# Layer 0 of a four-layer image network: four products behind one attention step, loads behind the first stacks, scales moved by two products

## The chip, the core and the metric

The kernel runs on one core of a Trainium2 chip. The metric is the device time of one execution in microseconds (us); three runs of the kernel before took 3771.85, 3773.90 and 3775.54, median 3773.9.

The engines are named as in the profile: PE (TensorE, matrix products; PEld are its weight loads), DVE (VectorE), ACT (ScalarE, functions such as exp and Gelu, which need a table loaded), POOL (GpSimd), SP (SyncE, which here only issues DMA transfers). ACT and POOL can issue DMAs too. Each engine works through its own instructions in their order; a semaphore wait at the head holds up all that stands behind it. Results of PE go to PSUM, of which this part of the kernel uses four single banks for products and two double ones for scores.

## The reference

Eight images of 384 channels and 32 x 32 pixels pass through four residual layers. Only layer 0 is touched:

```python
x = x + L0(_gn(x))                      # group norm over 32 groups
def L0(x):
    q = dwproj(x, dw_q, g_q, b_q, pw_q) # and k, v alike
    attn = softmax(einsum('bhcn,bhcm->bhnm', q, k) * scale)   # 8 heads of 48
    out  = einsum('bhnm,bhcm->bhcn', attn, v)
    return bn(einsum('oc,bchw->bohw', w_out, out))
def dwproj(x, dw, g, b, pw):
    y = depthwise 3x3 convolution of x with dw
    y = gelu(bn(y, g, b))               # bn: mean and variance over all 8 images
    return einsum('oc,bchw->bohw', pw, y)
```

The batch norm inside `dwproj` needs all eight images' convolutions before the first Gelu. That splits layer 0 into two stages.

## The kernel before

All arithmetic is in 32-bit floats. The program is traced into instructions for five engines; a scheduler orders them within each engine by readiness and priority, and every DMA is put on one of eight semaphores in turn, so that a new DMA waits for the one before it on the same semaphore (the profile shows this as SP or ACT waiting for a DMA).

**Stage A, convolutions (0 to 384 us).** Image `b` is loaded (`load_x`), normed (`norm`: statistics on DVE, two tiny products with `g4` on PE, a power on POOL) and written by ACT into a padded tile `pad`, two of which take turns. The 3 x 3 convolution of q, k and v at once is done on PE by groups of 42 channels: `stack` copies three row-shifted versions of a group's channels out of `pad` into a tile `st` (three SP DMAs of 168 KB; six of 24 KB for the group of leftover channels, number NGC = 9), and six products with the weights `cw` (or `cwr` for group 9) sum the taps in PSUM. `groups[b]` says which groups an image does on PE, group 9 first; for even images the last three groups are done tap by tap on DVE instead (`convolve`, tile `yv`). ACT copies the sums to `y`, DVE takes statistics (`bn_stats`), and ACT issues three stores of `y` to the DRAM tensors `raw`. `stacks(AHEAD)` issues stacks nine work items ahead. Image 1 is loaded before image 0's stacks in SP's queue; the constants `gb0`, `sel0`, `sel1`, `msk`, `one3` come behind image 2.

**The passage (384 to 400 us).** `bn_params` makes one scale and one shift per channel in the layout of the groups (126 partitions by group). Six small products with selection matrices `sel0` and `sel1` move them into the layout of the images (`pmove`, lines 416 and 420), DVE masks and sums them into `ss0` (lines 426 to 435), and ACT's first Gelus read `ss0`. Meanwhile the attention's weights are loaded (line 512), and POOL clears two tiles `vt` for the values (`values_tile`, line 505).

**Stage B, attention (400 to 1840 us).** A step is a pair of key tiles: for image `b`, head pair `pr` (four), half of the queries `h` (two) and key tiles `kc`, `kc+1` there are 32 steps an image. Each step issues the scores of the next step (16 rows of PE, line 623, four at a time in quarters of the array), their exps on ACT (line 630), the Gelus due for the next image (`GELUS`, by step), and the weighing of its own probabilities (`weigh`, line 638, in quarters too) into two banks `pav`. Other work waits in a list `todo`: projections of q and k (line 558), values (line 531), out-projections (line 575), which use the whole array, three products each (two rows of the profile per product). Two of them are done behind every second step:

```python
            if n % NS or (b == 0 and pr == 0 and h == 0):
                for _ in range(min(2, len(todo))):
                    todo.pop(0)()
            if kc == NT8 - NS:
                normalise(b, pr, h, pav)
```

`normalise` divides by the sums on DVE and puts the result into `att`; for the last head pair by 12 small DMAs. The order on ACT in this stage is the program's own (`manual_schedule`); the other engines' follows it closely.

Behind it, layers 1 to 3 run to 3770 us; nothing of them changes.

Of the kernel before, what the change touches and what calls it, by code (L numbers as in the profile page):

```python
# [1 line left out]

# [50 lines left out]
def tile_kernel(ctx: ExitStack, tc: tile.TileContext, i: dict, out: bass.AP):  # L53
# [13 lines left out]
    def bank(name):  # L67
        return ps_mm.tile([P, HALF], F32, tag="mm", name=name)
# [11 lines left out]
    def load_const(name):  # L80
        src = i[name]
        t = const.tile(list(src.shape), F32, tag=name, name=name + "_sb")
        nc.sync.dma_start(out=t, in_=src)
        return t

    ident = load_const("ident")
    g4 = load_const("g4")
    mhalf = const.tile([P, 16], F32, name="mhalf")
    nc.vector.memset(mhalf, -0.5)
    ones = const.tile([P, P], F32, name="ones")  # L90
# [128 lines left out]
    with ExitStack() as pa:  # L219
# [20 lines left out]
            load_image(xts[b], x_img[b])  # L240

        load_x(0)
        cwr = load_a("cwr")
        cw = load_a("cw")
        cwv = load_a("cwv")
        vst = wa.tile([3 * GC, 3, 2, 6], F32, name="vst")

        def norm(b):
# [62 lines left out]
        def stack(b, g):  # L311

            padf = pads[b % 2].rearrange("p c h w -> p c (h w)")
            if g < NGC:
                st = sa.tile([3 * GC, H, W], F32, tag="st", name=f"st{b}_{g}")
                c, t = divmod(g, 3)
                for dy in range(3):
                    nc.sync.dma_start(
                        out=st[dy : 3 * GC : 3].rearrange("p h w -> p (h w)"),
                        in_=padf[t : 3 * GC : 3, c, dy * W : (dy + H) * W],  # L320
                    )
            else:
                st = sa.tile([32 + 3 * GR, H, W], F32, tag="sr", name=f"st{b}_{g}", bufs=2)
                for h in range(2):
                    for dy in range(3):
                        r = 32 * h + dy * GR
                        nc.sync.dma_start(
                            out=st[r : r + GR].rearrange("p h w -> p (h w)"),
                            in_=padf[3 * GC :, :, dy * W : (dy + H) * W],
                        )  # L330
            return st
# [2 lines left out]
        TAPS = [(1, 0, W, 0), (0, 0, W - 1, 1), (2, 1, W, 0)]  # L334
        AHEAD = 9
        groups = [(NGC, *range(NGC - 3 if b in ON_V else NGC)) for b in range(B)]
        work = [(b, g) for b in range(B) for g in groups[b]]

        begins = {max(2, work.index((b, NGC)) - AHEAD - 2): b for b in range(1, B)}
        sts, taps, todo, later, normed = {}, [], {}, list(work), {0}  # L340

        def stacks(n):
            while later and len(work) - len(later) < n and later[0][0] in normed:
# [2 lines left out]

        for f in norm(0):
            f()
        stacks(AHEAD)
        load_x(1)  # L350
        load_x(2)
        gb0 = load_a("gb0")
        sel0, sel1, msk, one3 = (load_a(n) for n in ("sel0", "sel1", "msk", "one3"))
        for n, (b, g) in enumerate(work):
            if n in begins:
                b2 = begins[n]
# [32 lines left out]
            for v in range(3):  # L389
                if g < NGC:  # L390
                    to, of = raw[v][b, g % 3 : 3 * GC : 3, g // 3, :], y[v : 3 * GC : 3, :]
                else:
                    to, of = raw[v][b, 3 * GC :, :, :], y[v * GR : (v + 1) * GR, :]
                nc.scalar.dma_start(out=to, in_=of)
            for _ in range(2):
                if taps:
                    taps.pop(0)()
# [4 lines left out]
        assert not taps and not todo and not xts  # L402


        scs, shs = bn_params(gb0[:, 0, :], gb0[:, 1, :], bn0)
        both = wa.tile([3 * GC, 2, NGC + 1], F32, name="both")
        nc.vector.tensor_copy(both[:, 0, :], scs)
        nc.vector.tensor_copy(both[:, 1, :], shs)
        rest = wa.tile([3 * GR, 2, KC], F32, name="rest")
        nc.vector.tensor_tensor(  # L410
            rest, both[: 3 * GR, :, NGC:].to_broadcast([3 * GR, 2, KC]),
            one3.unsqueeze(1).to_broadcast([3 * GR, 2, KC]), ALU.mult,
        )
        pm = bank("pmove").rearrange("p (a v n) -> p a v n", a=2, v=4)
        for v in range(3):
            nc.tensor.matmul(
                pm[:, 0, v, : 2 * (NGC + 1)], lhsT=sel0[:, v, :],
                rhs=both.rearrange("p s g -> p (s g)"), start=True, stop=True,
            )
            nc.tensor.matmul(  # L420
                pm[:, 1, v, : 2 * KC], lhsT=sel1[:, v, :],
                rhs=rest.rearrange("p s k -> p (s k)"), start=True, stop=True,
            )
        got = wa.tile([P, 3, 2, KC, 3], F32, name="got")
        for v in range(3):
            nc.vector.tensor_tensor(
                got[:, v], pm[:, 0, v, : 2 * (NGC + 1)].rearrange("p (s g) -> p s g", s=2)[
                    :, :, :NGC
                ].rearrange("p s (k t) -> p s k t", t=3),
                msk.unsqueeze(1).unsqueeze(1).to_broadcast([P, 2, KC, 3]), ALU.mult,  # L430
            )
        nc.vector.reduce_sum(
            ss0.rearrange("p v s k -> p (v s k)"), got.rearrange("p v s k t -> p (v s k) t"), AX.X
        )
        nc.vector.tensor_tensor(
            ss0.rearrange("p v s k -> p v (s k)"), ss0.rearrange("p v s k -> p v (s k)"),
            pm[:, 1, :3, : 2 * KC], ALU.add,
        )

# [50 lines left out]
    with ExitStack() as pb:  # L492
# [9 lines left out]

        def values_tile(s):
            t = wb.tile([P, NT8, 2 * NH0, 32], F32, name=f"vt{s}")
            nc.gpsimd.memset(t, 0.0)
            nc.gpsimd.memset(t[:, :, :, HQ0 : HQ0 + 1], 1.0)
            vts.append(t)

        values_tile(0)
        for v, nm in enumerate(("wq0", "wk0", "wv0")):  # L510
# [1 line left out]
            nc.sync.dma_start(out=t, in_=i[nm])  # L512
            w_in.append(t)
        wo0 = wb.tile([P, KC, C], F32, name="wo0_sb")
        nc.sync.dma_start(out=wo0, in_=i["wo0"])
        rec = wb.tile([P, B * NU, 16], F32, name="rec")

        qks, atts = {}, {}
# [1 line left out]

        GELUS = {
            s: [divmod(i, KC) for i in range(2 * k, min(2 * k + 2, 3 * KC))]
            for k, s in enumerate((7, 9, 11, 13, 17))
        }

        def values(b, t):
            pv = bank(f"pv{b}_{t}")
# [39 lines left out]
        def out_project(b, m, h):  # L569
            hs = slice(h * HALF, (h + 1) * HALF)  # L570
            xh = op.tile([P, HALF], F32, tag="xh", name=f"xh{b}_{m}_{h}")
            nc.sync.dma_start(out=xh, in_=x_img[b][:, m, hs])
            po = bank(f"po{b}_{m}_{h}")
            for c in range(KC):
                nc.tensor.matmul(  # L575
# [94 lines left out]
        for n, (b, pr, h, kc) in enumerate(steps):  # L670
# [39 lines left out]
            for k in range(NS):  # L710
                weigh(b, pr, kc + k, pav, cur[k])

            if n % NS or (b == 0 and pr == 0 and h == 0):
                for _ in range(min(2, len(todo))):
                    todo.pop(0)()
            if kc == NT8 - NS:
                normalise(b, pr, h, pav)
# [1046 lines left out]
def _layouts(a):  # L1764
# [33 lines left out]
        gb[: 3 * GR, k, NGC] = v[:, NGC * GC :].reshape(-1)  # L1798
    L["gb0"] = gb

    sel = np.zeros((GC, 3, 3, P), f)
    for v in range(3):
        for t in range(3):
            sel[np.arange(GC), v, v, 3 * np.arange(GC) + t] = 1
    L["sel0"] = sel.reshape(3 * GC, 3, P)
    sel = np.zeros((3, P - 3 * GC, KC, 3, P), f)
    for v in range(3):
        for q in range(P - 3 * GC):
            sel[v, q, :, v, 3 * GC + q] = 1
    L["sel1"] = sel.reshape(3 * GR, 3, P)  # L1810
    row = np.arange(P)[:, None]
    L["msk"] = ((row % 3 == np.arange(3)) & (row < 3 * GC)).astype(f)
    L["one3"] = np.tile(np.eye(KC, dtype=f), (3 * GR // KC, 1))

    hrow = np.arange(C).reshape(NH0, HD0)
    rows = np.concatenate(
# [65 lines left out]
```

## Time and profile before

| What | us |
|---|---|
| median of three runs | 3773.9 |
| the profiled execution | 3772.1 |
| its span | 3770.3 |
| PE busy (97%) | 3647.7 |
| DVE busy | 1818.9 |
| ACT busy | 1316.8 |
| first convolution product starts | 21.9 |
| last convolution product ends | 384.5 |
| first projection starts | 400.4 |
| distance of images 1 to 6 in stage B | 177.4 |

In a line of the timeline stand start and duration in us, engine, line of the code, operation, output and inputs, number of instructions, and in brackets how long the engine had been idle and what released it. In a line of the waits: who waited for whom, total us, times, longest. A busy PE is not PE at its peak, since its rows overlap; the distance of starts tells more. The row PEclk is the clock granted to PE in tenths; at half speed a row of 512 columns starts 0.83 us behind the one before, at full speed 0.43.

### The profile page before, as it was taken

The page shows a single profiled execution, that of the slowest core. Times are in us where ns is not written, and L with a number is a line of the kernel's source. Part 1 is how long each engine was busy: PE and PEld are TensorE (multiplying, and loading weights), DVE is VectorE, ACT ScalarE, POOL GpSimd, SP SyncE. Part 2 cuts the span into 40 slices and gives each one's busy share as a digit, 9 for nine tenths or more (in the row PEclk, how much of TensorE's full clock was granted, in tenths as well). Part 3 has the DMA queues.
Part 4 walks back from the last instruction along what each step waited for, and adds up shares of the span by engine and source line. Part 5 has one row for each costly group of instructions (what it writes and reads, how often), then busy time and mean ns, then how long its engine had stood idle before and what let it go on. Part 6 is the DMA issues. An engine that isn't in the chain of part 4 may idle for free.

```text
span 3770.3 us, 39346 instructions
## 1 busy us (share of the span) xinstructions
PE 3647.7 (97%) x15754; PEld 1521.3 (40%) x15754; DVE 1818.9 (48%) x2841; ACT 1316.8 (35%) x1564; POOL 194.8 (5%) x153
## 2 busy tenths in 40 slices
PE   7999899999999999999799999999999999999898
PEld 3444333333333333333244534445444444444433
DVE  5876223232323232323346557565664666547664
ACT  2222364554545454534222321323222232322222
POOL 0000000000000000000000010200102010010111
PEclk9999999999999999999899999999999999999898
DMA  6777311111212020212340000100001001010000
GB/s 201 240 245 245 107 50 37 65 44 55 61 41 74 25 74 26 72 27 71 138 183 25 26 34 17 34 34 17 34 17 49 19 17 34 17 51 17 1 34 18
DMA packets 83097, 242.64 MB, mean 64 GB/s; under 512 B 18336, under 2 KB 18864, under 8 KB 82520
## 3 DMA queue, kind: packets, MB, share of 16 engines
q1 hardware_dynamic: 69894, 200.56, 16.1%
q10 hardware_dynamic: 13008, 39.43, 3.1%
q8 instruction: 128, 2.10, 0.2%
q14 instruction: 67, 0.55, 0.0%
HBM read 122.78 MB, written 75.50 MB: 53 GB/s over the span
## 4 chain that ended last, share of the span: by engine, by line
PE 40%; DVE 9%; ACT 1%; issue 0%; POOL 0%; DVEq 0%; POOLq 0%; ACTq 0%
PE y L1265 11%; PE ph L1244 8%; DVE y L1339 6%; PE pq L1384 3%; PE pw L1347 3%; PE pf L1650 3%; PE s L1545 3%; PE pav L1561 2%; PE pss L1587 1%; DVE hd L1230 1%; DVE off L1454 1%; PE pk L1519 1%; PE pv L1528 1%; PE xsb L1505 1%; PE plog L1007 1%; PE pom L1467 1%
## 5 line engine op out<-in xcount | busy, mean ns | idle before, releaser
L630 ACT ACTIVATE p<-s 128x1024 f32<-128x1024 f32 x512 | 496.4, 1021 | 496.9 <-PE s L623 496.5
L1265 PE MATMUL y<-hd,w_sb 128*128 128x512 f32 x1080 | 491.0, 600 | 3.6 <-DVE hd L1230 3.6
L638 PE MATMUL pav<-p,vt 64*64 64x512 f32 x4096 | 486.6, 590 | 0.0
L1244 PE MATMUL ph<-h,w_sb 128*128 128x512 f32 x1104 | 483.3, 594 | 0.0
L623 PE MATMUL s<-qk,qk 48*64 48x512 f32 x3072 | 372.7, 600 | 4.4 <-ACT p L630 4.4
L381 PE MATMUL pk<-st,cw_sb 126*126 126x512 f32 x720 | 316.4, 600 | 5.2 <-DVE ga_a L118 4.2
L1244 PEld LDWEIGHTS ph<-h,w_sb 128*128 128x128 f32 x1104 | 207.6, 190 | 253.1 <-issue 250.3
L1265 PEld LDWEIGHTS y<-hd,w_sb 128*128 128x128 f32 x1080 | 199.3, 191 | 249.8 <-issue 236.0
L638 PEld LDWEIGHTS pav<-p,vt 64*64 64x64 f32 x4096 | 156.2, 133 | 285.4 <-issue 285.1
L595 DVE COPY ta<-pav 128x512 f32<-128x512 f32 x64 | 44.3, 691 | 439.2 <-PE pav L638 439.2
L1339 DVE SCALAR_TENSOR_TENSOR y<-h,tap,y 128x992 f32<-128x992 f32 (+1 forms) x192 | 233.8, 1241 | 1.6
L1454 DVE SCALAR_TENSOR_TENSOR off<-q,dw_sb,off 128x225 f32<-128x225 f32 (+3 forms) x432 | 213.3, 549 | 1.7
L1254 ACT ACTIVATE hd<-ph,b_sb 128x512 f32<-128x512 f32 x180 | 122.7, 682 | 258.3 <-PE ph L1244 257.9
L381 PEld LDWEIGHTS pk<-st,cw_sb 126*126 126x126 f32 x720 | 137.6, 193 | 176.8 <-issue 167.8
L623 PEld LDWEIGHTS s<-qk,qk 48*64 48x64 f32 x3072 | 102.5, 132 | 241.5 <-issue 184.6
L78 DVE COPY qk<-pq 128x512 f32<-128x512 f32 x48 | 33.2, 691 | 293.6 <-PE pq L558 281.8
L387 ACT COPY y<-pk 126x512 f32<-126x512 f32 (+1 forms) x136 | 75.9, 584 | 250.7 <-PE pk L381 118.3
L1552 ACT ACTIVATE p<-s 128x1024 f32<-128x1024 f32 x96 | 93.1, 1021 | 173.4 <-PE s L1545 173.3
L575 PE MATMUL po<-att,wo_sb 128*128 128x512 f32 x288 | 135.7, 621 | 8.5 <-DMA att<-al 8.5
L1230 DVE TENSOR_TENSOR hd<-hd,cb 128x512 f32<-128x512 f32 x180 | 122.2, 684 | 35.4 <-ACT hd L1254 35.0
L1347 PE MATMUL pw<-y,upw 128*128 128x512 f32 x288 | 129.7, 603 | 7.6 <-DVE y L1339 7.6
L558 PE MATMUL pq<-g,wq_sb 128*128 128x512 f32 x288 | 132.8, 612 | 2.2 <-ACT g L483 2.2
(278 smaller groups left out, 4004.4 us busy)
## 6 DMA issues: line engine op xcount, KB each, us to landing
g<-raw SPq DMA_DIRECT2D x72, 512.0 KB
st<-pad SPq DMA_DIRECT2D x180, 168.0 KB
raw<-y ACTq DMA_DIRECT2D x180, 168.0 KB
xa<-in_x_dram SPq DMA_DIRECT2D x24, 512.0 KB
xh<-in_x_dram SPq DMA_DIRECT2D x48, 256.0 KB
f<-in_x_dram SPq DMA_DIRECT2D x24, 512.0 KB
f<-o SPq DMA_DIRECT2D x24, 512.0 KB
o<-ot SPq DMA_DIRECT2D x42, 256.0 KB
```

The costliest lines, as they stand in the source:

```text
L381: nc.tensor.matmul(pk[h].rearrange("p (h w) -> p h w", w=W)[: 3 * nch, :, o0 : o0 + c1 - c0], lhsT=lhs, rhs=rhs, start=(k == 0), stop=(k = ...
L558: nc.tensor.matmul(pq, lhsT=w_in[v][:, c, pr * P : (pr + 1) * P], rhs=acts[b][v][:, c, h * HALF : (h + 1) * HALF], start=(c == 0), stop=(c ...
L575: nc.tensor.matmul(po, lhsT=wo0[:, c, m * P : (m + 1) * P], rhs=atts[b][:, c, hs], start=(c == 0), stop=(c == KC - 1),)
L623: nc.tensor.matmul(s[64 * k : 64 * k + 64, j * HALF : (j + 1) * HALF], lhsT=kt[r, k0 : k0 + 64], rhs=qt[r, h * HALF : (h + 1) * HALF], sta ...
L630: nc.scalar.activation(p, s, AF.Exp, scale=scale)
L638: nc.tensor.matmul(pav[k][64 * j : 64 * j + 64, :], lhsT=vts[b % 2][r, kc, 2 * hd : 2 * hd + 2, :].rearrange("p a b -> p (a b)"), rhs=p[r, ...
L1230: nc.vector.tensor_tensor(hd, hd, state["cb"], ALU.mult)
L1244: nc.tensor.matmul(ph, lhsT=w1[:, e, c, dc * P : (dc + 1) * P], rhs=state["h1"][c], start=(c == 0), stop=(c == KC - 1),)
L1265: nc.tensor.matmul(y, lhsT=w2[:, e, dc, m * P : (m + 1) * P], rhs=state[h, k], start=(k == 0), stop=(k == NE * KC - 1),)
L1339: nc.vector.scalar_tensor_tensor(d, f, tap2[:, c, t : t + 1], d, ALU.mult, ALU.add)
L1347: nc.tensor.matmul(pw[h], lhsT=upw2[:, c, m * P : (m + 1) * P], rhs=y[c][:, hs], start=(c == 0), stop=(c == KC - 1),)
L1454: nc.vector.scalar_tensor_tensor(d, f, dw3[:, t : t + 1], d, ALU.mult, ALU.add)
```

## The change

- `ident` and `g4` are no longer loaded first. `g4` and the first third of `cw` come behind image 0, then `cwv` and `cwr`.
- Image 0 does groups 0, 1 and 2 before group 9. Image 1's load, the rest of `cw` and `ident` are held behind the first two groups' stacks (`issue_after`).
- `sel0`, `sel1` and `one3` have new contents, and `is_v` is new. In the changed program's order on SP, the small constants (`gb0`, `sel0`, `sel1`, `msk`, `is_v`, `one3`, and stage B's `gbo`, `gw`, `gbias`, `ewt`, `sel2`) stand before the first stack.
- The last image's groups 5, 6 and 7 are stored from POOL's queue, not from ACT's.
- Scales and shifts are spread over q, k and v by a mask on DVE (`both`, `rest`), and two products move all of them, instead of six.
- POOL's clearing of `vt` waits until the scales are done.
- The first image's loads `xh` wait behind `wo0`.
- Gelus of the next image come three at a time at steps 9, 13 and 17, not two at a time at 7, 9, 11, 13 and 17.
- Up to four items of `todo` are done behind the second of four steps; the very first unit keeps two behind each.

```diff
-    ident = load_const("ident")
-    g4 = load_const("g4")
...
         load_x(0)
+        g4 = load_const("g4")
+        cw = wa.tile([3 * GC, NGC, 3, 3 * GC], F32, name="cw_sb")
+        nc.sync.dma_start(out=cw[:, :3], in_=i["cw"][:, :3])
+        cwv = load_a("cwv")
         cwr = load_a("cwr")
-        cw = load_a("cw")
-        cwv = load_a("cwv")
...
-                    nc.sync.dma_start(
+                    stacked[0] = nc.sync.dma_start(
...
+        groups[0] = (*groups[0][1:4], NGC, *groups[0][4:])
...
+        stacks(2)
+        with tc.issue_after(stacked[0].ins):
+            load_x(1)
+            nc.sync.dma_start(out=cw[:, 3:], in_=i["cw"][:, 3:])
+            ident = load_const("ident")
         stacks(AHEAD)
-        load_x(1)
         load_x(2)
...
-                nc.scalar.dma_start(out=to, in_=of)
+                queue = nc.gpsimd if b == B - 1 and g in (5, 6, 7) else nc.scalar
+                queue.dma_start(out=to, in_=of)
...
+        both = wa.tile([3 * GC, 3, 2, NGC], F32, name="both")
+        rest = wa.tile([3 * GR, 3, 2, KC], F32, name="rest")
+        two = bn_params(gb0[:, 0, :], gb0[:, 1, :], bn0)
+        for k, t in enumerate(two):
+            sh = [3 * GC, 3, NGC]
+            nc.vector.tensor_tensor(
+                both[:, :, k], t[:, :NGC].unsqueeze(1).to_broadcast(sh),
+                is_v.unsqueeze(2).to_broadcast(sh), ALU.mult,
+            )
...
-        for v in range(3):
-            nc.tensor.matmul(
-                pm[:, 0, v, : 2 * (NGC + 1)], lhsT=sel0[:, v, :],
...
+        nc.tensor.matmul(
+            pm[:, :nv], lhsT=sel0, rhs=both.rearrange("p v s g -> p (v s g)"),
+            start=True, stop=True,
+        )
+        nc.tensor.matmul(
+            pm[:, nv : nv + 6 * KC], lhsT=sel1, rhs=rest.rearrange("p v s k -> p (v s k)"),
+            start=True, stop=True,
+        )
...
-            nc.gpsimd.memset(t, 0.0)
+            zero = nc.gpsimd.memset(t, 0.0)
+            tc.add_manual_dep(
+                zero.ins, scales.ins.name, mybir.DependencyInfo(
+                    mybir.DependencyClass.Sync, mybir.DependencyReason.DATA
+                ), reason="scales first",
+            )
...
-            s: [divmod(i, KC) for i in range(2 * k, min(2 * k + 2, 3 * KC))]
-            for k, s in enumerate((7, 9, 11, 13, 17))
+        GELUS = {s: [(v, c) for c in range(KC)] for v, s in enumerate((9, 13, 17))}
...
-            nc.sync.dma_start(out=xh, in_=x_img[b][:, m, hs])
+            with tc.issue_after(w_last.ins) if b == 0 else nullcontext():
+                nc.sync.dma_start(out=xh, in_=x_img[b][:, m, hs])
...
-            if n % NS or (b == 0 and pr == 0 and h == 0):
-                for _ in range(min(2, len(todo))):
+            early = b == 0 and pr == 0 and h == 0
+            if early or kc == NS:
+                for _ in range(min(2 if early else 4, len(todo))):
                     todo.pop(0)()
```

## The prediction

> **What bounds the kernel now.** First the page: span, engine totals, the slices.
>
> ```profile
> span 3770.3 us, 39346 instructions
> PE 3647.7 (97%) x15754; PEld 1521.3 (40%) x15754; DVE 1818.9 (48%) x2841; ACT 1316.8 (35%) x1564; POOL 194.8 (5%) x153
> ...
> PE   7999899999999999999799999999999999999898
> ...
> PEclk9999999999999999999899999999999999999898
> ```
>
> TensorE (PE) is busy throughout; the thin slices are the start, the passage from stage A to the attention (380 to 400 us) and two places behind it that the change leaves alone. So time comes from PE's waits, and from what PE does between waits. Second, PE's waits, longest first:
>
> ```profile
> PE gna_a L116 <- DVE mv_a L110: 11.4, 2, 10.2
> PE pmove L416 <- DVE both L408: 10.5, 1, 10.5
> PE pk L381 <- DMA st<-pad: 10.5, 2, 9.9
> PE po L575 <- DMA att<-al: 8.5, 4, 4.9
> ```
>
> Only some 40 us in all: two at the start, one in the passage, one at the attention's end. Third, the timeline of the first 31 us and of the passage:
>
> ```profile
> 4.56 1.39 SPq L171 DMA_DIRECT2D xa<-in_x_dram  x3
> 14.36 1.73 SPq L318 DMA_DIRECT2D st<-pad  x2
> 21.93 8.15 PE L381 MATMUL pk<-st,cwr_sb 18*18 18x512 f32 x12 [9.89 <-DMA st<-pad]
> ...
> 386.95 0.59 ACT L387 COPY y<-pk 126x512 f32<-126x512 f32 x1 [2.30 <-DMA raw<-y]
> ...
> 391.08 3.51 POOL L505 MEMSET vt<- 128x4096 f32 x1
> ...
> 391.46 3.16 DVE L407 COPY both<-bnsc_qkv 126x10 f32<-126x10 f32 x1
> ...
> 400.40 1.22 PE L558 MATMUL pq<-g,wq_sb 128*128 128x512 f32 x1 [2.16 <-ACT g L483]
> ```
>
> The first stack is issued at 14.36, but image 1 (4.56) and the 1.7 MB of `cw` stand before it in SP's queue: the queue's packets finish with image 1 at 18.66, and only then does the stack move. In the passage, a 126x10 copy that takes 0.17 elsewhere takes 3.16, as long as POOL's memset beside it. Fourth, PE inside the attention:
>
> ```profile
> 1007.18 2.00 PE L623 MATMUL s<-qk,qk 48*64 48x512 f32 x16
> 1009.00 1.90 PE L638 MATMUL pav<-p,vt 64*64 64x512 f32 x16
> 1010.83 5.42 PE L575 MATMUL po<-att,wo_sb 128*128 128x512 f32 x12
> 1016.18 1.95 PE L623 MATMUL s<-qk,qk 48*64 48x512 f32 x16
> ```
>
> There is no wait, yet starts are not evenly spaced. Scores and weighing run as quartets 0.429 apart, full products 0.429 apart. From the rows' single starts: last weighing quartet to first full product 0.538, that one to the second 0.534, last full product to scores 0.522, first score quartet to the second 0.480. Against even spacing, one change to full products and back costs 0.109 + 0.105 + 0.093 + 0.051 = 0.358 us, the same to 0.01 in the 93 batches from 480 to 1780 us (values' products, 0.323 apart, show the same surplus).
>
> **The change part by part.** *Four products behind one step.* Work is equal; only the number of batches falls. In the changed program's order of PE they go from 102 to 59: six fewer in each of images 1 to 6, four in image 0, three in image 7. 36 x 0.358 = 12.9 for images 1 to 6. Elsewhere scores that follow weighing directly lie at 0.429, so nothing returns. The exception is behind Gelu batches: scores two steps later start at 0.51 with two quartets at 0.48, 0.187 together. Gelu batches fall from five to three: 6 x 2 x 0.187 = 2.2. Together 15.1. The bounds: all new successions late leaves 36 x 0.171 = 6.2; none late gives 18.5.
>
> Banks: `pav` holds two of four, so the third product needs the first one's bank. The second product's 2.57 us covers one 0.69 evacuation, even behind a Gelu batch. Four out-products need 4 x 2.8 of DVE (copy 0.69, statistics 0.69, 0.73, 0.69), 11.2 against PE's 10.3; the third still finds its bank.
>
> *Gelu in threes.* ACT's rows in image 0:
>
> ```profile
> 470.58 1.28 ACT L483 ACT_TABLE_LOAD   x1
> 471.88 2.37 ACT L483 ACTIVATE g<-g,ss 128x1024 f32<-128x1024 f32 x2
> 474.27 1.28 ACT L630 ACT_TABLE_LOAD   x1
> ```
>
> A batch costs 2 x 1.28 + 3 x 1.18 = 6.1 instead of 4.9. Behind a batch of products (5.2 us or more) it is covered. Image 0's fourth unit has none: there PE waited 2.25 before, and with three Gelus I get 2.25 + 1.2 = 3.5. But the batch at 470 moves to a step with four products, so its wait of 2.1 to 2.3 and the half-speed products behind it (7.15 with the other wait) fall away. I give back half the slow phase (1.3): 7.15 - 3.5 - 1.3 = 2.3, lateness 0.2, four batches 1.4: image 0 saves 3.9.
>
> *Image 7.* Three batches fewer, -1.1. But its third early out-product ran after the last weighing (1823.07, 2.84 us), while PE waited for `att` until 1830.86. Now it comes before that weighing, so the last normalisation starts 2.6 later: +1.5 net. Attention: -15.1 - 3.9 + 1.5 = -17.5.
>
> *Loads behind the first stacks.* Without `ident` ahead and with `g4` behind, image 0 arrives 0.9 earlier, so `pad`'s first chunk is ready at 13.4; three stack DMAs go out 0.8 apart, and the last lands 2.4 after issue (40.67 to 43.08 shows that on an empty queue): 17.6, 4.3 earlier. Image 1, two thirds of `cw` and `ident` (2.8 MB, 8.5 us at the 330 GB/s seen here) now precede the third stack: it lands near 30.9, when two groups are done: 0.9 of waiting. Group 9 needs a bank that ACT frees behind a store of `yv`, whose taps DVE finishes near 39.5: another 1.5. Bounds of this feeding: 0 and 6.
>
> At the start products run at 0.83, half speed, from 21.93 to 34.20, costing 5.1. *The Trainium skill*, "TensorE: Matmul & The Clock Gate", Part 1, says that full clock comes after one busy window of about 3.4 us; by the rule the cold cost would be 1.7, by the row 5.1, for products with 18 rows. The phase from 400.40 to 406.3, with full products, is nearer to what now starts: 5.9 us, 2.9 lost. I take that: -2.2.
>
> Eleven small loads (`gb0` to `sel2`) are now issued before the first stack, in SP's idle time. Before, five held SP from 49.75 to 57.9 while image 1's stacks waited, and PE lost 7.1 between 63 and 78 us (starts against 0.43: waits of 2.3, then slow clock). I credit 2 of it, bounds 0 and 7. Stage A: -4.3 - 2.2 + 2.4 - 2.0 = -6.1.
>
> *The passage.* PE's last product ends at 384.45. ACT's last copy waited behind stores until 386.95: with three groups' stores on POOL it starts at 384.7 (-2.25). The memset now waits for the scales, so DVE's 3.1 stall goes (-3.0); four fewer move products x 0.53 and one `got` instead of three, less two more small DVE operations: -1.5. The first product comes at 393.65, 6.75 earlier; I take -6.7. Weights must be there: `wq` landed at 394.28, but was issued at 390.14, after the last of six `g` loads had landed; now it is queued right behind them and should land near 391. If not, 0.6 is lost. The memsets end near 400, the first `vt` copy needs them at 409: covered. `xh` behind `wo0`: needed only in image 1, free.
>
> Nine stores on POOL: no row shows one. The skill's "SBUF — State Buffer" (the "DVE blocks DMA" trap) speaks against it: descriptors of such a DMA can't be written while DVE holds a shared port, 0.62 becoming 3.1 us. Three stores of the last group queue before POOL's power (387.0 in the new chain): at 1 us each they are out by 383, by the rule at 3.1 each 390, a loss of 3. DVE's rows here are statistics of 0.69 and 0.57, no copies; I take no loss and keep 3 for the range.
>
> Sum: -6.1 - 6.7 - 17.5 = -30.3. The profiled execution took 3772.1, its span 3770.3; the median is 3773.9. From the median: **3743.6 us**.
>
> **Rivals.** *The stacks eat the head start*: the third one and the bank cost 6, the boundary gains nothing: -24, 3750. For it: SP waits for ACT's stores already at 33.43 and 40.67; against: no PE wait there so far. *The switch is dear only where a wait stands*: new successions late: -9 less, and POOL's stores cost 3: -18, 3755. For it: the 0.51 rows; against: all those follow Gelus. *The boundary clears wholly*: -36, 3738. *Slower*: a merged batch's third product waits for its bank because DVE's copy stands behind the 2.8 us chain of the one before. From 0.7 us per batch on (43 x 0.7 = 30) the gain is gone; at a full 1.4 it is 3774 - 30 + 60 = 3804. Against: 2.57 of cover. *Nothing moves*: PE's time is products alone, and the gaps come back elsewhere: 3773.
>
> **How the numbers follow.** Likeliest 50% (alone 3737 to 3749), stacks 18%, dear switch 13%, boundary 14%, slower 3%, nothing 2%. The range 3735 to 3756 takes in the first four. 0.2% (7.5 us) is about what a measurement of this kernel can tell from no change: faster 0.95, same 0.02, slower 0.03.
>
> **What would show it.** First stack product near 17.6; first `pq` about 13 before 400.4; no 3 us copy beside the memset; images 1 to 6 174.9 us apart instead of 177.39; 12 or more rows between weighing and scores doubled to 24 with the same 0.358. Wrong if PE waits for `st` or banks before 60 us, if POOL's power comes late, or if merged batches show a gap inside.

## The result, and the profile after

The changed kernel takes 3751.11 us (median, 3749.07 to 3757.77) where the kernel before takes 3772.88: a ratio of 0.9948, 95% interval 0.993 to 0.9967. It is faster by about 20 us, not by the 30.3 of the sum. Its profiled execution took 3751.05, its span is 3749.3, 21.0 under the 3770.3 before; the points below are made on these two spans. First the page's span and PE's rows of the slices:

```profile
span 3749.3 us, 39325 instructions
PE 3632.0 (97%) x15746; PEld 1533.0 (41%) x15746; DVE 1820.6 (49%) x2840; ACT 1280.2 (34%) x1536; POOL 199.5 (5%) x162
...
PE   7999999999999999999799999999999999999888
...
PEclk8999999999999999999899999999999999999898
```

The busy products fell by only 16 us of 3648. PE's waits of the changed kernel:

```profile
PE gna_a L114 <- DVE mv_a L108: 14.2, 2, 9.0
...
PE po L590 <- DMA att<-al: 11.6, 4, 7.9
PE pk L391 <- DMA st<-pad: 10.2, 3, 7.2
```

The passage's wait of 10.5 is gone from the top of this list. The wait for the first stack is 7.2 instead of 9.9, but there are now three such waits instead of two, and the wait of `gna_a` for `mv_a`, which was 11.4, has grown to 14.2, 5.2 of it late in stage A. The timeline of the changed kernel, start and passage:

```profile
13.16 4.90 SPq L318 DMA_DIRECT2D st<-pad  x6
18.00 12.85 PE L391 MATMUL pk<-st,cw_sb 126*126 126x512 f32 x24 [7.17 <-DMA st<-pad]
18.11 1.51 SPq L169 DMA_DIRECT2D xa<-in_x_dram  x3
22.63 8.10 SPq L318 DMA_DIRECT2D st<-pad  x3
32.95 6.98 PE L391 MATMUL pk<-st,cw_sb 126*126 126x512 f32 x12 [2.10 <-DMA st<-pad]
...
387.75 0.58 ACT L397 COPY y<-pk 126x512 f32<-126x512 f32 x1 [1.94 <-PE pk L391]
...
392.29 0.18 DVE L423 TENSOR_TENSOR both<-bnsc_qkv,is_v_sb 126x27 f32<-126x27 f32 x1
...
396.36 8.18 PE L572 MATMUL pq<-g,wq_sb 128*128 128x512 f32 x12 [2.20 <-DMA wq_sb<-in_wq_dram]
```

The first stack product comes at 18.00 (before 21.93). PE waits for the third stack at 32.95, and its next twelve products take 6.98 instead of 5.3. At stage A's end ACT's last copy follows PE directly, `both` takes 0.18, and the first `pq` comes at 396.36 (before 400.40). And one place in the attention (image 3):

```profile
997.38 1.90 PE L653 MATMUL pav<-p,vt 64*64 64x512 f32 x16
999.20 5.42 PE L590 MATMUL po<-att,wo_sb 128*128 128x512 f32 x12
1004.46 5.31 PE L572 MATMUL pq<-g,wk_sb 128*128 128x512 f32 x12
1009.70 1.95 PE L638 MATMUL s<-qk,qk 48*64 48x512 f32 x16
```

Two out-products and two projections now stand in one batch; the 24 rows run without a gap, so the third product finds its bank.

Against the sum, on the profiled spans:

| part | predicted | measured | from |
|---|---|---|---|
| stage A, start of its last product | -6.1 | +3.3 | 383.87 to 387.13 |
| passage, from there to the first `pq` | -6.7 | -7.3 | 16.53 to 9.22 |
| first `pq` to first scores | 0 | -0.05 | 15.24 to 15.19 |
| first scores to `gmean` (layer 0 over) | -17.5 | -15.9 | 1431.31 to 1415.41 |
| behind it | 0 | -1.1 | 1923.39 to 1922.32 |

One line carries nearly all of the miss: stage A.

### The profile page after: what moved, and what is told of

Same layout as the page of the kernel before. It is cut to its first block, busy times and chain, and to the rows that moved or that the text cites. A ratio compares the mean times of both kernels' runs of the same rounds, so it can differ in the third digit from the quotient of the medians.

```text
span 3749.3 us, 39325 instructions
## 1 busy us (share of the span) xinstructions
PE 3632.0 (97%) x15746; PEld 1533.0 (41%) x15746; DVE 1820.6 (49%) x2840; ACT 1280.2 (34%) x1536; POOL 199.5 (5%) x162
## 4 chain that ended last, share of the span: by engine, by line
PE 40%; DVE 9%; ACT 1%; issue 0%; DMA 0%; POOL 0%; DVEq 0%; POOLq 0%; ACTq 0%; SPq 0%
PE y L1281 11%; PE ph L1260 8%; DVE y L1355 6%; PE pq L1400 3%; PE pw L1363 3%; PE pf L1666 3%; PE s L1561 3%; PE pav L1577 2%; PE pss L1603 1%; DVE hd L1246 1%; DVE off L1470 1%; PE pk L1535 1%; PE pv L1544 1%; PE xsb L1521 1%; PE pom L1483 1%; PE plog L1023 0%
## 5 line engine op out<-in xcount | busy, mean ns | idle before, releaser
L590 PE MATMUL po<-att,wo_sb 128*128 128x512 f32 x288 | 132.8, 615 | 11.6 <-DMA att<-al 11.6
```

What stands on the lines that cost most here:

```text
L590: nc.tensor.matmul(po, lhsT=wo0[:, c, m * P : (m + 1) * P], rhs=atts[b][:, c, hs], start=(c == 0), stop=(c == KC - 1),)
```

## The experiments

Each ratio is to runs of the kernel before on the same chip, whose medians lay between 3772.9 and 3777.2 us; times of kernels that ran on different chips are best compared by their ratios. "Last product" is the start of stage A's last product; the passage runs from there to the first `pq`; the attention from the first scores to `gmean`. All in us, each from one profiled execution; the ratio is that of the timed runs.

| kernel | first product | last product | passage | attention | ratio to before, 95% |
|---|---|---|---|---|---|
| before | 21.93 | 383.87 | 16.53 | 1431.31 | |
| after | 18.00 | 387.13 | 9.22 | 1415.41 | 0.9948 (0.993, 0.9967) |
| e1 attention alone | 21.93 | 382.18 | 16.97 | 1415.55 | 0.9953 (0.994, 0.9967) |
| e2 passage alone | 21.83 | 382.75 | 10.10 | 1431.13 | 0.9978 (0.9969, 0.9987) |
| e3 start alone | 18.20 | 385.94 | 15.29 | 1429.79 | 0.9998 (0.9989, 1.0006) |
| e4 after, old start | 22.05 | 381.43 | 9.06 | 1415.05 | 0.9927 (0.9913, 0.994) |
| e5 after, four stacks first | 18.33 | 380.36 | 9.06 | 1414.36 | 0.9929 (0.9916, 0.9943) |
| e6 after, tail and Gelu moved | 18.19 | 385.50 | 9.38 | 1395.97 | 0.9893 (0.9877, 0.9908) |
| e7 after, stores on ACT | 18.53 | 387.75 | 11.41 | 1414.21 | 0.9944 (0.9929, 0.9959) |
| e8 after, memset free | 18.32 | 389.56 | 9.06 | 1414.13 | 0.9938 (0.9923, 0.9954) |
| e9 batches alone | 22.23 | 386.69 | 16.82 | 1459.11 | 1.0066 (1.005, 1.0083) |
| e10 before, copies as products | 22.40 | 390.18 | 14.47 | 1433.36 | 0.999 (0.9981, 0.9998) |
| e11 e6 with the old start | 22.21 | 383.78 | 9.06 | 1395.60 | 0.9886 (0.987, 0.9903) |
| e12 e6 with four stacks first | 18.75 | 382.31 | 9.06 | 1395.49 | 0.9885 (0.9869, 0.9902) |

### Which part brings what: e1 to e4

Attention alone (e1), on the kernel before:

```diff
-            s: [divmod(i, KC) for i in range(2 * k, min(2 * k + 2, 3 * KC))]
-            for k, s in enumerate((7, 9, 11, 13, 17))
+        GELUS = {s: [(v, c) for c in range(KC)] for v, s in enumerate((9, 13, 17))}
...
-            if n % NS or (b == 0 and pr == 0 and h == 0):
-                for _ in range(min(2, len(todo))):
+            early = b == 0 and pr == 0 and h == 0
+            if early or kc == NS:
+                for _ in range(min(2 if early else 4, len(todo))):
```

> The kernel before with two edits alone: up to four products behind one step of four, and Gelu in threes. If the cost of a change to full products and back is what the batches save, images 1 to 6 last 174.88 us each instead of 177.39 (-15.1 in all), image 0 saves 1.6 to 3.9 and the tail loses 1 to 1.5: time near 3773 - 16 to -17.5, 3756. If the switch is dear only where a wait stands, images last about 176.4 and the time is near 3764.

Measured 3755.53 against 3777.2. Images 1 to 6 last 174.89 each, the attention 15.8 less. The theory holds; the rival of a dear switch is out.

Passage alone (e2): the scales by two products, the memset's wait, the nine stores on POOL, as in the change.

> The kernel before with the passage's edits alone: scales by two products, the memset behind the scales, nine stores on POOL. The theory: last conv product to first pq falls from 15.95 to about 8.7 us, stage A's end does not move, time near 3773 - 7 = 3766. The rival, that POOL's stores hold up its power: the passage falls by 4 only, 3769.

Measured 3766.39; the passage is 10.10 (in this profile PE waited 3.1 for `wq`; it is 9.06 in the profiles where `wq` was there in time). The theory holds: 6.4 of some 7, and POOL's stores cost nothing.

Start alone (e3):

```diff
-    ident = load_const("ident")
-    g4 = load_const("g4")
...
+        groups[0] = (*groups[0][1:4], NGC, *groups[0][4:])
...
+        stacks(2)
+        with tc.issue_after(stacked[0].ins):
+            load_x(1)
+            nc.sync.dma_start(out=cw[:, 3:], in_=i["cw"][:, 3:])
+            ident = load_const("ident")
         stacks(AHEAD)
-        load_x(1)
```

> The kernel before with the start's edits alone: loads behind the first stacks, group 9 fourth, cw in two parts. The theory: the first product comes 3.9 us earlier, but the wait for the third stack and the image boundaries, which run in another planned order on DVE, ACT and SP, give back more than that: stage A's last product ends 3 us later than in the kernel before (near 387.7), time near 3776. The rival of the prediction: the head start lasts, the last product ends near 378.5 and the time is near 3767. A third: the loss belongs to another edit, and this one ends near 381.

Measured 3775.07 against 3777.2: no difference, within -4 and +2. The last product starts 2.1 later than in the profile of the kernel before, though the first one comes 3.7 earlier. The prediction's own figure (3767) is out. The expected loss of 3 did not show in the time: the profiled execution was the fastest of 13, its passage and first projections were 2.6 shorter than in the kernel before, and why is not known.

The changed kernel with these edits undone (e4):

> The changed kernel with the start's edits undone. The theory: stage A's last product ends at 384.4 as in the kernel before, 3.3 us earlier than in the changed kernel; time near 3751 - 3 = 3748. The rival, that the start's edits are worth 6 us as predicted: near 3757.

Measured 3747.67, 0.9927: not slower than the changed kernel, so the start's edits are not worth 6 us there either. Attention and passage alone add to 26.1 by their ratios, and e4 saves 27.6. The start adds nothing that these times can show.

### Where the head start goes: e5, and all profiles side by side

Stage A wanders between executions, so I took all profiles with the same start together: seven with the old one, five with the new (after, e3, e6, e7, e8), two with four stacks first. Mean start of the n-th product of stage A (12 to a group), and the new start's lead over the old:

| product | old | new | new - old | four - old |
|---|---|---|---|---|
| 1st | 22.08 | 18.25 | -3.8 | -3.5 |
| 19th | 34.57 | 28.05 | -6.5 | -6.3 |
| 25th (third stack) | 37.09 | 33.39 | -3.7 | -6.3 |
| 37th (group 9, new start) | 42.28 | 39.66 | -2.6 | +1.7 |
| 61st | 52.67 | 52.35 | -0.3 | +3.9 |
| 85th (image 1) | 63.95 | 63.70 | -0.3 | +3.0 |
| 97th | 73.87 | 70.12 | -3.7 | -2.9 |
| 145th | 96.26 | 92.53 | -3.7 | -2.7 |
| 193rd | 118.71 | 119.22 | +0.5 | -2.0 |
| 481st | 240.08 | 240.49 | +0.4 | -1.9 |
| 577th | 285.87 | 288.82 | +3.0 | -2.6 |
| last | 384.41 | 387.18 | +2.8 | -3.1 |

Up to the 241st product the standard deviation within the old and the new start is 0.2 to 1.5 us; at the end it is 3.0 (old) and 1.6 (new), so the last row alone would prove little. The rows above it show where the lead is spent: 2.8 at the third stack, 1.1 of slow clock behind that wait, 2.3 around group 9, then 3.5 won at the border to image 1, 4.2 lost near product 170 and 2.5 near product 577.

At the last two PE's `gna_a`, the small product in the norm of the next image but one, waits for that image's statistics on DVE. In DVE's timeline of the changed kernel near 280 us, image 7's statistics (`st_a`, six, then `mv_a`) stand among taps of image 6:

```profile
276.98 1.29 DVE L103 BATCH_NORM_STATS2 st_a<-xa 128x6 f32<-128x512 f32 x2 [7.43 <-DMA xa<-in_x_dram]
...
278.62 1.28 DVE L103 BATCH_NORM_STATS2 st_a<-xa 128x6 f32<-128x512 f32 x2
279.82 0.73 DVE L290 TENSOR_SCALAR yv<-xn,cwv_sb 126x1024 f32<-126x1024 f32 x1
...
284.55 0.68 DVE L103 BATCH_NORM_STATS2 st_a<-xa 128x6 f32<-128x512 f32 x1
285.15 1.20 DVE L292 SCALAR_TENSOR_TENSOR yv<-xn,cwv_sb,yv 126x961 f32<-126x961 f32 x1
...
288.06 0.30 DVE L108 BATCH_NORM_AGGREGATE mv_a<-st_a 128x2 f32<-128x36 f32 x1
```

Four taps and five statistics of products stand between the first `st_a` and `mv_a`, 11.1 us in all; `gna_a` waits 5.2 us at 288.50. The diff has no line there: the planner, given another start, put DVE's work in another order. With the old start the six stand together and take 5.5 to 7.0 from the first to `mv_a`, and `gna_a` waits 0.3 at most; in all five profiles with the new start they take 10.8 to 12.2, and it waits 4.4 to 7.5. At image 3 (product 170) the new order puts `mv_a` behind two more of image 0's taps, and the wait is 2.4 to 4.3 instead of 1.2 to 1.7.

It is tempting to call this order the cause, but at image 7 the old start pays one step later. Its PE passes `gna_a` and then waits 1.6 to 5.6, in six profiles for `ga_a`, which DVE makes of that product, and in one (e9) for a store. PE in e10, with the old start, and in the changed kernel:

```profile
285.62 0.35 PE L116 MATMUL gna_a<-mv_a,g_sb 128*128 128x2 f32 x2
291.60 7.14 PE L381 MATMUL pk<-st,cw_sb 126*126 126x512 f32 x12 [5.63 <-DVE ga_a L118]
...
288.50 0.56 PE L114 MATMUL gna_a<-mv_a,g_sb 128*128 128x2 f32 x2 [5.18 <-DVE mv_a L108]
```

Between products 481 and 625 PE waits 4.7 us in the mean with the old start and 5.6 with the new; the clock is at half speed for 7.8 and 13.0 us. Between products 145 and 193 it waits 1.3 and 3.5, at half speed for 0.5 and 5.5. So at image 3 about half of the loss is longer waiting, at image 7 less than half; the rest is slow clock.

What goes with the loss at image 7 in all 14 profiles is how late its data come. Take the time from the start of the 529th product to the image's first statistics, ahead of which DVE waits for the load in every profile. It is 8.4 to 11.6 us in six profiles (four with the old start, e5 and e12), and products 481 to 625 take 63.8 to 66.2 there. It is 12.5 to 16.5 in the other eight, and they take 66.6 to 70.4: 67.9 to 69.1 in the three with the old start and its statistics together (e9, e10, e11), 66.6 to 70.4 in the five with the new start and its statistics among taps. With data equally late, the old order loses as much as the new one. Why the data come late is not shown.

At image 3 order and load change together. SP issues the load at 94.2 in the mean with the new start and at 95.0 with the old: 0.8 earlier, where PE is 3.7 ahead, because the load stands on SP behind `cst<-vst`, which waits for stores of convolution results.

With four stacks first (e5) the planner's order has image 7's statistics together again:

```diff
-        stacks(2)
+        stacks(4)
         with tc.issue_after(stacked[0].ins):
-            load_x(1)
             nc.sync.dma_start(out=cw[:, 3:], in_=i["cw"][:, 3:])
+            load_x(1)
```

> The changed kernel with the stacks of its first four groups ahead of image 1, and the rest of cw ahead of image 1 too. In the changed kernel the wait for the third stack and the slow clock behind it cost 4 us, and late in stage A the planner put four taps and four groups' statistics between the statistics of the last image on DVE, which made PE wait 5.2 us near 288 us and run slowly behind it, 7 us in all; here those statistics stand together again. The theory: both waits go, stage A's last product starts near 378 to 381 instead of 387.1, and the time is 5 to 8 us below the changed kernel's. The rival, that DMA landings alone pace stage A's later images whatever the order: 385 or later, and no gain.

Measured 3746.27 (0.9929); last product at 380.36, and 382.31 in e12. DVE's timeline of e5 at the same place:

```profile
269.13 0.69 DVE L103 BATCH_NORM_STATS2 st_a<-xa 128x6 f32<-128x512 f32 x1 [6.43 <-DMA xa<-in_x_dram]
...
272.09 1.28 DVE L103 BATCH_NORM_STATS2 st_a<-xa 128x6 f32<-128x512 f32 x2 [1.08 <-DMA xa<-in_x_dram]
...
273.64 1.28 DVE L103 BATCH_NORM_STATS2 st_a<-xa 128x6 f32<-128x512 f32 x2
274.96 0.32 DVE L108 BATCH_NORM_AGGREGATE mv_a<-st_a 128x2 f32<-128x36 f32 x1
```

5.8 us instead of 11.1, and no wait of `gna_a`, but 2.4 for `ga_a` behind it; image 7's first data also came 2.4 us earlier against PE's progress than in the changed kernel, so this run does not single out the order. Where the new start loses 4.2 and 2.5 against the old one, e5 gains 0.6 at image 3 and e12 loses 2.2, and neither loses at image 7. The place holds: the lead is lost where the next image's load and statistics come late. At image 3 these runs don't separate the order on DVE from the load's place on SP. That e5 gains nothing from its early third stack is the other half of the lesson: image 1 lands later, PE waits 7.8 us for its statistics at 42.98, and a lead of 6.3 becomes a lag of 3.9 by the 61st product.

### The passage: e7, e8, e10

The nine stores back on ACT (e7): `nc.scalar.dma_start(out=to, in_=of)` for all groups.

> The changed kernel with the nine stores of the last image's groups 5, 6 and 7 back on ACT's queue instead of POOL's. The prediction took 2.25 us of the passage from these (ACT's last copy waits for its stores): last conv product to first pq grows from 9.2 to about 11.4, time 2 us above the changed kernel's. The rival, that POOL's stores cost as much as they save: 9.2 stays or falls.

Measured: passage 11.41 instead of 9.22. The 2.25 of the prediction is 2.2. The time, 3751.97, can't resolve it.

The memset without its wait (e8): `tc.add_manual_dep(...)` left out.

> The changed kernel with POOL's memset of vt free to start when it can, without its wait for the scales. The prediction took 3.0 us from this wait: DVE's copies beside the memset should take 3 us or more again, and last conv product to first pq grows from 9.2 to about 12.2. The rival, that the other short form of the scales has no operation beside the memset that suffers: 9.2 stays.

Measured: passage 9.06. The expected stall did not come back; the rival holds. POOL and DVE in e8:

```profile
394.37 6.95 POOL L516 MEMSET vt<- 128x4096 f32 x2
...
394.72 0.18 DVE L423 TENSOR_TENSOR both<-bnsc_qkv,is_v_sb 126x27 f32<-126x27 f32 x1
```

The memset started just ahead of the four small products into `both` and `rest`, and these took 0.15 to 0.19 each beside it. So the wait for the scales, which the prediction credited with 3.0, does nothing here. Is it the form of the operation? In the kernel before (e10):

```diff
-        nc.vector.tensor_copy(both[:, 0, :], scs)
-        nc.vector.tensor_copy(both[:, 1, :], shs)
+        one = ones[: 3 * GC, : NGC + 1]
+        nc.vector.tensor_tensor(both[:, 0, :], scs, one, ALU.mult)
+        nc.vector.tensor_tensor(both[:, 1, :], shs, one, ALU.mult)
```

> The kernel before, its two copies into both written as products by ones (same values, two inputs from SBUF). The memset on POOL still starts when it can. The theory from the run with the memset free: the 3.16 us stall belongs to the copy, and a product beside the memset takes its 0.15 to 0.19: last conv product to first pq falls from 16.5 by 3, time near 3773 - 3. The rival, that any DVE operation beside the memset waits for it: the first product into both takes 3 us, nothing is gained.

Measured: 0.999 (0.9981 to 0.9998), passage 14.47. The timeline of e10, POOL and DVE:

```profile
398.23 3.51 POOL L506 MEMSET vt<- 128x4096 f32 x1
...
398.61 0.16 DVE L408 TENSOR_TENSOR both<-bnsc_qkv,ones 126x10 f32<-126x10 f32 x1
```

The product takes 0.16 beside the same memset where the copy took 3.16. (In the kernel before, a product issued 0.12 behind that copy took 3.04; it ended with the copy, and e10 shows that it was the copy that held it.) From DVE's first operation on the last group's moments (`bnsh`) to the first `pq` it is 8.6 instead of 11.5: 2.9 saved by the form alone. *The Trainium skill*, "SBUF — State Buffer", section "SBUF: two separate sides", says this: a DVE operation in a two-port mode, which a 32-bit copy within SBUF is said to bring about, or one with two inputs from SBUF, takes the port pair it shares with GpSimd, the latter only against a GpSimd operation that reads SBUF. A memset reads nothing; the trace agrees, 3.16 and 0.16.

### The attention: e6, e9

Two edits in the changed kernel (e6): image 7's early out-products behind the last weighing, and image 0's Gelus at other steps.

```diff
-            if early or kc == NS:
+            last = (b, pr, h) == (B - 1, NPAIR0 - 1, 1)
+            if early or (kc == NS and not last):
...
-        GELUS = {s: [(v, c) for c in range(KC)] for v, s in enumerate((9, 13, 17))}
+        GELUS = [
+            {s: [(v, c) for c in range(KC)] for v, s in enumerate(at)}
+            for at in ((9, 17, 21), (9, 13, 17))
+        ]
```

> The changed kernel with two edits in the attention: image 7's three early out-products all behind the last weighing, and in image 0 the second and third Gelu batch at steps 17 and 21, which have products, instead of 13 and 17. If image 0's missing gain is the wait at its fourth unit with the slow phase behind it (3.4 and 2.9 us), its length falls from 178.66 to about 173.5. If the early out-products hold up the last normalisation by their whole time, 15.2 us from the weighing before them to the scores behind, first score to the end of layer 0 falls by about 13 at the tail: 1415.4 to 1397, time near 3733. The rivals: ACT and DVE now evacuate six products at the end and give back 5 or more there; Gelu at 21 delays the values' products and image 0 stays above 176.

Measured 3732.57 (0.9893). Image 0 lasts 172.52 instead of 178.66: the wait and the slow phase behind it were 6.1 us. (In e5, e7 and e8, with the same Gelus as the changed kernel, it lasts 177.4, since the clock is at half speed for 3.4 us behind that wait and not for 6.8.) From the start of image 7 to `gmean` it is 174.21 instead of 187.45, 13.2 less, as worked out. PE's timeline at the end, the changed kernel and then e6:

```profile
1785.26 1.10 PE L590 MATMUL po<-att,wo_sb 128*128 128x512 f32 x2 [1.55 <-DMA att<-al]
1787.85 2.07 PE L590 MATMUL po<-att,wo_sb 128*128 128x512 f32 x2 [1.49 <-DMA att<-al]
1790.62 8.22 PE L590 MATMUL po<-att,wo_sb 128*128 128x512 f32 x14 [0.70 <-DMA att<-al]
1798.78 1.95 PE L638 MATMUL s<-ql,ql 48*64 48x512 f32 x16
1800.54 3.62 PE L653 MATMUL pav<-p,vt 64*64 64x512 f32 x32
1812.03 9.48 PE L590 MATMUL po<-att,wo_sb 128*128 128x512 f32 x18 [7.88 <-DMA att<-al]
```

```profile
1777.61 3.60 PE L656 MATMUL pav<-p,vt 64*64 64x512 f32 x32
1781.15 8.89 PE L593 MATMUL po<-att,wo_sb 128*128 128x512 f32 x20
1790.57 7.10 PE L593 MATMUL po<-att,wo_sb 128*128 128x512 f32 x16 [0.53 <-DMA att<-al]
```

The waits for `att` (11.6) fall to 0.5: the early products now fill the time in which the last normalisation and its DMAs run. ACT and DVE give back 3.0 of it ahead of `gmean` (a wait of 8.3 instead of 5.3). Behind `gmean` e6 takes 2.3 us longer than the changed kernel (1924.63 against 1922.32; e11 and e12 are alike), so some 11 of the 13.2 are left at the end.

Batches of four with Gelu left in twos (e9): the second hunk of e1 alone.

> The kernel before with up to four products behind one step of four, and Gelu still in twos (five batches). The prediction's split of an image's 2.52 us: six fewer changes to full products and back at 0.358 each, 2.15, and two fewer Gelu batches at 0.187, 0.37. So images 1 to 6 should last 177.39 - 2.15 = 175.24 us here, against 174.88 with Gelu in threes. The rival, that the batches of Gelu are worth nothing and the switch costs 0.42: 174.88 here too.

Measured 3799.56, 1.0066: slower than the kernel before, which neither theory foresaw. The timeline of e9, ACT and PE in image 2:

```profile
832.80 1.28 ACT L483 ACT_TABLE_LOAD   x1
834.10 2.37 ACT L483 ACTIVATE g<-g,ss 128x1024 f32<-128x1024 f32 x2
836.49 1.28 ACT L630 ACT_TABLE_LOAD   x1
...
838.86 3.68 PE L623 MATMUL s<-qk,qk 48*64 48x512 f32 x16 [2.13 <-ACT p L630]
842.29 3.62 PE L638 MATMUL pav<-p,vt 64*64 64x512 f32 x16
```

Steps 7 and 11 had products before and have none now; ACT's 4.9 us there lie bare. PE waits 2.1, fifteen times in the attention (31.4 us), and the scores and weighing behind such a wait take twice their time (3.68 and 3.62 for sixteen products, which take 1.95 and 1.90). Images 1 to 6 last some 181 in the mean instead of 175.24 (a few records are missing here). Gelu's move to steps 9, 13 and 17 is thus not the 2.2 us that I gave it: it is what keeps the batches' gain from turning into a loss of 24.

### Together: e11, e12

> The changed kernel with the start's edits undone, image 7's early out-products behind the last weighing, and image 0's Gelus at steps 9, 17 and 21. If the three parts add up, 29.5 below before without the start, and 18.5 more: near 3728. The rival, that stage A's end wanders by 2 us whatever the start: 3726 to 3732.

Measured 3731.06 (0.9886).

> The same with the start that puts four groups' stacks and the rest of cw ahead of image 1, instead of the old start. If the run with four stacks repeats (stage A's last product starting near 380.4) and the parts add up: near 3746.3 - 18.5 = 3728; PE waits 8 us for image 1's statistics near 43 us again, and not near 288. The rival, that its stage A was a lucky draw: 384 and 3732.

Measured 3730.41 (0.9885, 0.9869 to 0.9902), last product at 382.31. The parts add up to within 3 us, and e11 and e12 both beat the changed kernel by some 20. Between e6, e11 and e12, three starts with the rest alike, the times do not differ beyond their intervals.

## Why the prediction was right, and where it was not

The time, 3751.1, lies in the range and 7.5 above the forecast, outside the likeliest case (3737 to 3749); the range held because it took in the rivals. On the spans the sum missed 9.3: stage A by 9.4, the attention by 1.6, against 0.6 and 1.1 won in the passage and behind layer 0. The terms show why.

- **Start, -4.3 and -2.2.** Right: -3.8 at the first product and 2.7 of slow clock by the 19th, means of five and seven profiles. The row of a cold phase with full products, which I took, was the right one.
- **Feeding, +2.4.** This is the term that failed first: +6.2, just over its own bound of 6. The third stack cost 2.8 and not 0.9, since SP took 8.1 us over its three DMAs (22.63) and it was there at 32.95, not at 30.9. The slow clock behind the wait cost 1.1, which I had not priced. The bank's wait of 1.5 did not come; group 9's slow clock (below) did, 2.3, though the prediction had seen 18-row products at half speed for 12 us at the start.
- **Image border, -2.0.** Under by a little: -3.5 in the mean, though in the changed kernel's own profile it is 0. That the small loads brought it is not shown: PE's waits there in the kernel before were 1.5 for ACT's `y` and 0.8 for `ga_a`, none for a stack.
- **"Stage A: -6.1".** The step that failed is that this sum ends there. It took the rest of stage A as moved along rigidly. But 4.2 and 2.5 us went in two places where the next image's data and statistics come late against PE: at image 3 its load stands on SP behind other waits and does not follow PE's lead, and DVE has two more taps ahead of the statistics; at image 7 the data come late, whatever DVE's order. Longer waits and the slow clock behind them share the loss. With them stage A ends 2.8 later in the mean, not 6.1 earlier. The times of e3 show no gain either: the start alone saves 0.8, between 4.2 saved and 2.3 lost.
- **Passage, -6.7.** Right, -7.3. Its 2.25 for ACT's copy is 2.2 (e7). Its 3.0 for the memset's wait has the right size and the wrong owner: it is the copies' disappearance (e8, e10). `wq` came when needed to within 0.2 us here; in e2 it came 1.0 late. POOL's stores took 0.5 us each and lost nothing to DVE: 3 of the range not needed.
- **Images 1 to 6, -15.1.** Right: 1064.64 to 1049.30, -15.3. The split into 12.9 and 2.2 isn't shown: e9 can't isolate it.
- **Image 0, -3.9.** Over by 2.3. The wait was foreseen (3.5; 3.3 measured at 505.14), but the slow phase behind it is 2.9, not half of an old one: waits and slow phases together were some 6 before and are some 6 now, so only the four batches count; in e5, e7 and e8 the slow phase is shorter and image 0 saves 2.8. e6 shows the 6.1 by taking them away.
- **Image 7, +1.5.** Right: +1.05.

Of the rivals, "the stacks eat the head start" (3750) is what came in time; its mechanism covers half, the third stack and no more, since the bank cost nothing and the border did gain; so its hit is in part luck. "Dear switch", "third product waits for a bank" and "POOL's stores" are out.

The 1.1 us behind layer 0 were forecast as 0. Some 0.8 of them are slow clock: about 104 us behind `gmean` PE waits 3.57 for `hd` in both kernels, and then runs at half speed for 6.9 us before and 3.5 after (length; busy time of PE, PEld, DVE, ACT and POOL; clock; DMA share; GB/s):

```profile
1948.90:1955.80 6.90, 5.24 (x7) 2.19 (x8) 6.90 (x12) 2.06 (x3) 0.00 (x0) 0.51 0.00 0
...
1931.10:1934.60 3.50, 3.50 (x6) 1.46 (x5) 3.50 (x7) 1.63 (x2) 0.00 (x0) 0.51 0.00 0
```

In the 14 profiles the stretch behind `gmean` is 1922.3 to 1922.7 wherever this phase is the short one, and 1923.4 or more wherever it is the long one; what sets its length is not shown.

## What to carry to other kernels

A head start is worth what is left of it at the next place where two chains meet; follow it through every such place before it is added to a sum, and ask at each whether the other chain, here the next image's load and statistics, comes earlier too. Before products are gathered into fewer batches, list what ran under each old batch: here the gathering without Gelu's move costs 24 us, with it it gains 16 to 18. And work that is ready early belongs in the last wait of a chain: three products moved behind the last weighing were worth 13 us up to the end of layer 0 and some 11 in all, with no work removed.

## What the runs showed of the hardware

TensorE's clock fell to half with no idle time in the 8 us before, as far as the profile shows. In e3, group 9 stands fourth, behind full groups; busy times and granted clock by stretch, columns as above:

```profile
34.00:38.60 4.60, 4.60 (x13) 2.06 (x12) 4.53 (x8) 0.00 (x0) 0.00 (x0) 1.00 0.23 61
38.60:42.10 3.50, 3.50 (x12) 0.78 (x11) 3.40 (x8) 1.07 (x2) 0.00 (x0) 1.00 0.68 204
42.10:49.50 7.40, 7.30 (x12) 2.54 (x11) 1.68 (x5) 3.75 (x5) 0.55 (x1) 0.54 0.71 230
```

The first two rows show PE busy throughout; the products of 38.65 to 45.2 have 18 rows and 18 columns, and from 3.5 us into them the mean clock is 0.54 over 7.4 us. In each of the five profiles with the new start a slow phase begins in or right behind this group. *The Trainium skill*, "TensorE: Matmul & The Clock Gate", Part 1, lets the clock fall after an idle window; here a busy PE with small products had the same fate, and the measurement decides. In the old start this group ran first, while the clock was low anyway; moving it to the fourth place bought a slow phase. The kernel before shows the same at image 2, whose group 9 starts at 123.40, straight behind full products:

```profile
116.00:123.40 7.40, 7.40 (x18) 3.01 (x17) 2.93 (x5) 3.81 (x5) 0.00 (x0) 1.00 0.54 171
123.40:126.20 2.80, 2.80 (x14) 0.69 (x14) 2.73 (x4) 0.66 (x2) 0.00 (x0) 1.00 0.81 271
126.20:129.60 3.40, 3.40 (x5) 1.38 (x6) 3.40 (x4) 1.08 (x2) 0.00 (x0) 0.50 0.78 266
```

Over all 14 profiles 74 slow phases begin in stage A more than 15 us behind its first product. In 38 of them PE waited less than 0.7 us in the 7 us before, and every one of the 38 begins within a group 9 or at most 1.9 us behind the start of its last product, in stretches that make up about a ninth of that time. Not every such group has one: in the kernel before they stand at images 1 (with waits), 2 and 4, and not at 3, 5, 6 and 7. What decides is not shown.

The change from weighing to full products and back, 0.358 us, fits 2.51 us saved per image, for six of them (2.15) and two Gelu batches fewer (0.37); the two shares were not measured apart. And a small copy on DVE waited for a whole memset on POOL, while products with two inputs did not (3.16 and 0.16).
